# Setup loads on another queue, a first batch computed in pairs of halves, and a convolution split into more and smaller stages

## The chip, the cores and the metric

The kernel runs on one core of a Trainium2 chip. The metric is the device time in microseconds of one execution (us). The core has a matrix engine (PE, with a separate row PEld for its weight loads), a vector engine (DVE), a scalar engine (ACT), a general engine (POOL, GpSimd) and a queue engine (SP) that here only issues transfers (DMAs).

## The reference

The input is x of shape 32 × 96 × 56 × 56 (batch, channel, row, column), all in fp32. Two blocks follow each other.

```python
# block 0
h = depthwise_conv_7x7(x) + conv_b
h = layernorm over channels(h) * ln_g + ln_b
h = gelu(h @ w1 + b1) @ w2 + b2
x1 = h * layer_scale + x
# block 1: two Mamba layers along L = 56*56 tokens of a batch
for i in range(2):
    h = layernorm(seq); xs, z = split(h @ in_w)           # 96 -> 2 x 192
    xc = silu(causal 4-tap conv(xs))
    dt, B, C = split(xc @ xproj_w)                        # 6, 16, 16
    delta = softplus(dt @ dt_w + dt_b)
    state[d, s] = exp(delta*A) * state + delta*B*xc       # scan over tokens, 192 x 16 states
    y = (sum over s of state*C + D*xc) * silu(z)
    seq = seq + y @ out_w
gp = relu(mean of x1 over the picture @ gp_w.T + gp_b)
out = fus_w @ concat(seq, gp) + fus_b
out = batchnorm(out) over batch and picture; return out + x1
```

## The kernel before, in words

The work falls into a prologue, a main part of 256 stages and an epilogue.

**First convolution.** `b0` batches are convolved before the main part starts. `conv_pair(p)` does two channels at a time: a DMA on SP's queue (L160) brings the rows of both channels with all `b0` batches into one of three `xpads`, seven `copy_predicated` of DVE (L165) write a banded 112 × 112 matrix for each of seven column shifts, PE multiplies (L176, two groups of batches with seven taps each), ACT adds the bias (L180), and DMAs store the result in `conv_d[0]` (L184) and the bands in `band_d` (L170), for later use. Three pairs are issued, then the setup of the weights (L189 to L319), then the other 45 pairs. The setup's loads are DMAs on SP's queue: `column`, `blocks` and single ones. Outside the main part a scheduler orders the instructions of each engine; the queue of an engine is served in order.

**First batch.** `block0(0, c, s)` gives the pieces of block 0 for half `s` of chunk `c` (a chunk is 784 tokens, a half 392; four chunks make a batch): `load`, `load_x`, `center` (L365), `square` (L370), `mean` (L375), `root` (L381 and L382: a logarithm and an exponential on ACT), `norm` (L429, DVE), `up` (L434), `gelu` (L442), `down` (L449, L453), `residual` (L460). Each piece has a slot number. For batch 0 these pieces are issued by a sorted list in which each half starts three slots after the one before. Tiles of this part come from a pool with 3 buffers a name and 8 PSUM buffers. ACT's functions come in table sets; `exp_ln_tables()` (L361) preloads the set that has both exponential and logarithm.

**Main part.** A stage is one layer, one batch, one chunk, and the order of the stages alternates between the two layers. It has 24 steps, one for each block of 32 channels (6) and group of states (4). In each step DVE scans (L920), ACT makes the decays (L871), DVE or POOL the inputs (L913, L897), POOL multiplies by C (L924), and PE sums over states into `y` (L957); `spread` (L886, PE) copies `u` to all partitions and `gate` (L938, DVE) multiplies by `z`. The order on PE, ACT, DVE, POOL and SP is written out by hand: `put` places each piece at a slot of a stage and `run` issues it behind, or within, the step of that number. Beside the scan a stage carries the preparation of the next stage (`prep`), the end of the last one (`post`), one half of block 0 for a later batch (`block0`, in stages 2 to 249), and one piece of the remaining convolution: `conv(g, p)`, channel pair p of group g of `NB` batches, in the stages from 2 on. Its first `PARTS` entry has its seven taps (L541) at slots 7.7 to 10.4, the second at slots 18.5 to 22.2; the results are copied by ACT (L554) and stored.

Of the kernel before, what the change touches and what calls it, by code (L numbers as in the profile page):

```python
# [44 lines left out]
C = 96  # L45
# [16 lines left out]
def convnext_mamba_kernel(  # L62
# [31 lines left out]
    nc = tc.nc  # L94
    B = x.shape[0]
# [2 lines left out]
    const = ctx.enter_context(tc.tile_pool(name="const", bufs=1))  # L98


    NB = 7
    b0 = B - 3 * NB if B > 3 * NB else B
    groups = [(0, b0)] + [(b, b + NB) for b in range(b0, B, NB)]
    conv_d = [
        dram.tile([C * H, (hi - lo) * W], F32, name=f"conv_d{lo}", tag=f"conv_d{lo}")
# [18 lines left out]
    for dh in range(7):  # L124
        m = cc.tile([R2, R2], F32, name="m", tag="m", bufs=2)
# [25 lines left out]
    for i in range(3):  # L151
        t = cc.tile([R2, 7, R2], F32, name=f"band{i}", tag=f"band{i}")
        nc.gpsimd.memset(t, 0.0)
        bands.append(t)
        t = cc.tile([R2, b0, W + 6], F32, name=f"xpad{i}", tag=f"xpad{i}")
# [49 lines left out]
    for a in range(2):  # L205
        r = slice(64 * a, 64 * a + 64)
# [12 lines left out]

    def column(src, n, name):  # L220
        t = const.tile([n, 1], F32, name=name, tag=name)
        nc.sync.dma_start(t, src)
        return t

    def blocks(src, name):

        n = src.shape[1]
        t = const.tile([128, NQ, n], F32, name=name, tag=name)
        for a in range(2):
            nc.sync.dma_start(t[64 * a : 64 * a + 64], src.rearrange("(q m) n -> m q n", m=64))  # L230
        return t

    g0, be0 = column(ln0_g, C, "g0"), column(ln0_b, C, "be0")
    b2ls, lsc = column(b2, C, "b2ls"), column(lscale, C, "lsc")
    nc.vector.tensor_tensor(b2ls, b2ls, lsc, ALU.mult)
    b1_sb = const.tile([128, NF], F32, name="b1_sb")
    w2_sb = const.tile([128, NF, C], F32, name="w2_sb")
    ls = su.tile([128, C], F32, name="ls", bufs=1)
    nc.sync.dma_start(ls, lscale.rearrange("c one -> one c").partition_broadcast(128))
    for f in range(NF):  # L240
        nc.sync.dma_start(b1_sb[:, f : f + 1], b1[f * 128 : (f + 1) * 128, :])
        nc.sync.dma_start(w2_sb[:, f, :], w2[f * 128 : (f + 1) * 128, :])
        nc.vector.tensor_tensor(w2_sb[:, f, :], w2_sb[:, f, :], ls, ALU.mult)
    gpw_sb = const.tile([C, C], F32, name="gpw_sb")
    nc.sync.dma_start(gpw_sb, gp_wt)
    gpb = column(gp_b, C, "gpb")
    fw1 = const.tile([C, C], F32, name="fw1")
    nc.sync.dma_start(fw1, fus_wt[0:C, :])
    fw2 = const.tile([C, C], F32, name="fw2")
    nc.sync.dma_start(fw2, fus_wt[C : 2 * C, :])  # L250
    fusb = column(fus_b, C, "fusb")
    bng, bnb = column(bn_g, C, "bng"), column(bn_b, C, "bnb")

# [3 lines left out]
    def norm_weights(dst, src, g, b):  # L257


        n = src.shape[1]  # L260
        raw = su.tile([C, n], F32, name="raw", tag="raw")
        nc.sync.dma_start(raw, src)
        m = su.tile([C, C + 1], F32, name="m", tag="nm")
        nc.vector.tensor_scalar(m[:, 0:C], center_m, g, None, ALU.mult)
        nc.vector.tensor_copy(m[:, C : C + 1], b)
        ps = sups.tile([128, 512], F32, name="ps", tag="nps")
        nc.tensor.matmul(ps[0 : C + 1, 0:n], m, raw, start=True, stop=True)
        nc.vector.tensor_copy(dst, ps[0 : C + 1, 0:n])

    norm_weights(w1_sb, w1, g0, be0)  # L270
    for i in range(2):
        d = {}
        lg, lb = column(ln_g[i], C, f"lg{i}"), column(ln_b[i], C, f"lb{i}")
        wz = const.tile([C + 1, 2 * DIN], F32, name=f"inw{i}", tag=f"inw{i}")
        norm_weights(wz, in_w[i], lg, lb)
        wx = const.tile([C + 1, 4, DIN], F32, name=f"wx{i}", tag=f"wx{i}")
        nc.sync.dma_start(wx, taps[i].partition_broadcast(C + 1))
        for k in range(4):
            nc.vector.tensor_tensor(wx[:, k, :], wx[:, k, :], wz[:, 0:DIN], ALU.mult)
        d["wx"], d["wz"] = wx, wz[:, DIN : 2 * DIN]  # L280
        d["cb"] = blocks(mconv_b[i], f"cb{i}")
        d["xp"] = blocks(xproj_w[i], f"xp{i}")
        d["ow"], d["res"] = blocks(out_w[i], f"ow{i}"), eye
        if i == 1:

            d["res"] = fw1
            for q in range(NQ):
                ps = sups.tile([128, 512], F32, name="ps", tag="nps")
                nc.tensor.matmul(
                    ps[0:C, 0:64], d["ow"][0:64, q, :], ident[0:64, 0:64], start=True, stop=True  # L290
                )
                owt = su.tile([C, 64], F32, name="owt", tag="owt")
                nc.vector.tensor_copy(owt, ps[0:C, 0:64])
                ps = sups.tile([128, 512], F32, name="ps", tag="nps")
                for a in range(2):
                    nc.tensor.matmul(
                        ps[64 * a : 64 * a + 64, 0:C], owt, fw1, start=True, stop=True
                    )
                nc.vector.tensor_copy(d["ow"][:, q, :], ps[:, 0:C])
        d["dtb"] = blocks(dt_b[i], f"dtb{i}")  # L300
        dtw = const.tile([DTR, DIN], F32, name=f"dtw{i}", tag=f"dtw{i}")
        nc.sync.dma_start(dtw, dt_w[i])
        d["dtw"] = dtw
        dcol = blocks(dp[i], f"dp{i}")
        d["D"] = const.tile([128, NQ, 128], F32, name=f"D{i}", tag=f"D{i}")
        for q in range(NQ):
            nc.vector.tensor_scalar(d["D"][:, q, :], ident, dcol[:, q, :], None, ALU.mult)

        ar = su.tile([128, 2 * NQ, NS], F32, name="ar", tag="ar")
        A = const.tile([128, 2 * NQ, NG], F32, name=f"A{i}", tag=f"A{i}")  # L310
        for s in range(4):
            r = slice(32 * s, 32 * s + 32)
            nc.sync.dma_start(ar[r], a_log[i].rearrange("(q m) n -> m q n", m=32))
            nc.scalar.activation(A[r], ar[r, :, s::4], AF.Exp)
        nc.vector.tensor_scalar(A, A, -1.0, None, ALU.mult)
        d["A"] = A
        d["st"] = const.tile([128, 2 * NQ, NG], F32, name=f"st{i}", tag=f"st{i}")
        lay.append(d)
# [5 lines left out]
    for k in range(2):  # L324
        t = const.tile([C + 1, 3 + CH], F32, name=f"hn{k}", tag=f"hn{k}")
        nc.vector.memset(t[C : C + 1, :], 1.0)
        hns.append(t)
        t = const.tile([C + 1, HC], F32, name=f"hz{k}", tag=f"hz{k}")
# [8 lines left out]
    with ExitStack() as main:  # L337
        pre = []
# [6 lines left out]
        def work(shape, name, bufs):  # L345

            pool, n = (pre[0], 3) if pre else (wp, bufs)
            return pool.tile(shape, F32, name=name, tag=name, bufs=n)
# [10 lines left out]
        def exp_ln_tables():  # L359

            nc.scalar.preload_act_table_set("natural_log_exp_and_others")  # L361
# [16 lines left out]
        def rsqrt(ps):  # L378

            rs = ps[0:C, 0:HC]  # L380
            nc.scalar.activation(rs, rs, AF.Ln, bias=eps_c[0:C])  # L381
            nc.scalar.activation(rs, rs, AF.Exp, scale=-0.5)  # L382
# [10 lines left out]
        def block0(b, c, s):  # L393
# [3 lines left out]
            def load():  # L397
                if k == 0:
                    batch_sums[b] = work([C, NCH * 2], "sums", 2)
                v["cv"] = work([C, ROWS, W], "cv", 1)  # L400
                g = 0 if b < b0 else 1 + (b - b0) // NB
                at = (b - groups[g][0]) * W
# [20 lines left out]
                v["ps"] = mean_of(v["sq"], 2)  # L423

            def root():
                rsqrt(v["ps"])

            def norm():
# [10 lines left out]
            def gelu():  # L439
                v["gl"] = work([128, NF, HC], "gl", 1)  # L440
                for f in range(NF):
                    nc.scalar.activation(  # L442
                        v["gl"][:, f], v["pss"][f][:, 0:HC], AF.Gelu, bias=b1_sb[:, f : f + 1]
                    )
                exp_ln_tables()

            def down():
                v["ps"] = psum(2)
# [29 lines left out]
            def fuse():  # L478
# [11 lines left out]
            return last + [  # L490
                (-6, load), (2, load_x), (11.3, center), (12.1, square), (12.4, mean),
                (12.8, root), (14.1, True, norm), (15.6, up), (15.9, gelu), (17.3, down),
                (18.3, residual),
            ]


        with tc.tile_pool(name="p0", bufs=1) as p0, tc.tile_pool(
            name="pp0", bufs=1, space=PSUM
        ) as pp0:
            pre += [p0, pp0]  # L500
            pieces = [
                (slot + 3 * (2 * c + s), piece)
                for c in range(NCH)
                for s in range(2)
                for slot, *_, piece in block0(0, c, s)
            ]
            for _, piece in sorted(pieces, key=lambda p: p[0]):
                piece()
            pre.clear()

        wp = main.enter_context(tc.tile_pool(name="wp", bufs=2))
# [5 lines left out]

        xpad = wp.tile([R2, NB, W + 6], F32, name="xpad", tag="xpad", bufs=1)
        nc.vector.memset(xpad, 0.0)

        PARTS = (0, (NB + 1) // 2), ((NB + 1) // 2, NB)

# [504 lines left out]
    with tc.tile_pool(name="sp", bufs=1) as sp:  # L1027
        n = B * NCH
# [21 lines left out]
    with tc.tile_pool(name="fin", bufs=4) as fin:  # L1050
        for b in range(B):
            for a in range(2):
# [3 lines left out]
                r = fin.tile([C, 2 * CH], F32, name="fr")  # L1056
# [63 lines left out]
```

## Time and profile before

| | |
|---|---|
| three runs | 17344.25 us median, 17338.93 to 17366.62 |
| the profiled execution | 17343.56 us, span 17341.9 us |
| busy share of the span | PE 89%, DVE 93%, ACT 66%, POOL 90% |
| mean granted clock of PE | 0.932 |
| first scan / last scan ends | 574 us / 16980 us |

A row of the profile's groups names line, engine, operation, output and inputs, then busy time and mean duration. PE records two instructions for each fp32 matmul. Times in a timeline are from the start of the span.

### The profile page before, as it was taken

How to read it: one execution, taken by the hardware profiler on the slowest of the kernel's cores; microseconds unless marked ns; L12 is line 12 of the kernel's file. 1: busy time of each engine (PE TensorE's matmuls, PEld its weight loads, DVE VectorE, ACT ScalarE, POOL GpSimd, SP SyncE). 2: the span in 40 equal slices, each digit the busy share in tenths (PEclk: the TensorE clock that was granted, in tenths of full speed). 3: DMA queues.
4: the chain of work that ended last, by engine and by line, in shares of the span. 5: the costliest groups of instructions: out<-in, count | busy, mean ns of one | idle time of the engine just before them, and what ended most of it. 6: DMA issues, size and time to landing. Idle time of an engine off the chain costs nothing. (4 is left out here: it accounts for less than half of the span.)

```text
span 17341.9 us, 217468 instructions
## 1 busy us (share of the span) xinstructions
PE 15452.2 (89%) x67992; PEld 5467.0 (32%) x67992; DVE 16061.7 (93%) x12345; ACT 11459.0 (66%) x18648; POOL 15637.1 (90%) x8737
## 2 busy tenths in 40 slices
PE   8899999999999999999999988888888888888870
PEld 5233333333333333333333322222222222222220
DVE  8699999999999999999999999999999999999994
ACT  1666666666676776666666666666666666666653
POOL 0699999999999999999999999999999999999991
PEclk9899999999999999999999999999999999999985
DMA  4455555555555555555555555555555555555548
GB/s 107 105 138 140 139 136 139 139 140 140 133 141 140 140 140 135 138 140 140 137 136 141 137 129 125 124 131 127 124 126 128 128 125 124 131 128 125 127 113 280
DMA packets 1421981, 2346.44 MB, mean 135 GB/s; under 512 B 629958, under 2 KB 793586, under 8 KB 1420820
## 3 DMA queue, kind: packets, MB, share of 16 engines
q1 hardware_dynamic: 1413652, 2294.00, 53.5%
q10 hardware_dynamic: 7168, 38.54, 0.6%
q8 instruction: 536, 8.78, 0.2%
q14 instruction: 625, 5.12, 0.1%
HBM read 1929.11 MB, written 402.41 MB: 134 GB/s over the span
## 5 line engine op out<-in xcount | busy, mean ns | idle before, releaser
L924 POOL TENSOR_TENSOR da<-h,bc 128x784 f32<-128x784 f32 x6144 | 11295.2, 1861 | 799.0 <-DVE h L920 686.1
L920 DVE TENSOR_TENSOR_SCAN h<-da,st,w 128x784 f32<-128x784 f32 x3072 | 5664.2, 1844 | 324.0 <-ACT st L931 9.4
L957 PE MATMUL y<-da,ssum 128*32 128x392 f32 x24576 | 5131.2, 540 | 429.9 <-POOL da L924 427.5
L913 DVE TENSOR_TENSOR w<-w,bc 128x784 f32<-128x784 f32 x4096 | 3995.7, 976 | 284.0 <-PE w L886 114.6
L897 POOL TENSOR_TENSOR da<-us,bc 128x784 f32<-128x784 f32 x2048 | 3816.3, 1863 | 2.9 <-DMA us<-uu 2.9
L871 ACT ACTIVATE da<-d,A 128x784 f32<-128x784 f32 x4096 | 3757.6, 941 | 43.6 <-DMA d<-dd 27.7
L871 ACT ACTIVATE w<-d,A 128x784 f32<-128x784 f32 x2048 | 1878.8, 918 | 2662.8 <-DVE h L920 2270.2
L920 DVE TENSOR_TENSOR_SCAN h<-w,st,da 128x784 f32<-128x784 f32 x1536 | 2712.4, 1827 | 5.9 <-ACT w L871 4.8
L622 PE MATMUL ps<-hn,wx 97*64 97x392 f32 x12288 | 2262.6, 503 | 7.9 <-DVE hn L610 7.9
L957 PEld LDWEIGHTS y<-da,ssum 128*32 128x32 f32 x24576 | 1093.7, 115 | 3700.0 <-issue 2095.1
L920 DVE TENSOR_TENSOR_SCAN h<-da,w 128x784 f32<-128x784 f32 x1024 | 1827.0, 1784 | 107.9 <-ACT st L931 3.8
L886 PE MATMUL w<-u,sel 64*128 64x392 f32 x4096 | 1028.4, 581 | 638.5 <-DVE h L920 637.4
L622 PEld LDWEIGHTS ps<-hn,wx 97*64 97x64 f32 x12288 | 795.3, 136 | 1429.1 <-issue 1111.3
L701 POOL TENSOR_TENSOR u<-dl,xc 128x784 f32<-128x784 f32 (+1 forms) x512 | 736.8, 1439 | 543.0 <-ACT dl L687 543.0
L951 PE MATMUL y<-xc,D 128*128 128x392 f32 x1536 | 796.6, 604 | 252.1 <-DVE z L938 246.1
L541 PE MATMUL ps<-xpad,band 112*112 112x224 f32 (+1 forms) x4032 | 1003.0, 358 | 0.0
L361 ACT ACT_TABLE_LOAD x759 | 973.8, 1283 | 14.5 <-PEq L1107 0.8
L370 ACT ACTIVATE sq<-ps 96x392 f32<-96x392 f32 x768 | 340.7, 490 | 812.6 <-PE ps L365 464.3
L920 DVE TENSOR_TENSOR_SCAN h<-w,da 128x784 f32<-128x784 f32 x512 | 872.3, 1766 | 0.0
L541 PEld LDWEIGHTS ps<-xpad,band 112*112 112x112 f32 x4032 | 583.8, 175 | 832.5 <-issue 783.5
L679 PE MATMUL ps<-dbl,dtw 6*64 6x392 f32 x3072 | 688.3, 511 | 99.9 <-ACT dbl L657 99.9
L886 PEld LDWEIGHTS w<-u,sel 64*128 64x128 f32 x4096 | 327.7, 196 | 1229.6 <-DVE h L920 1055.3
(124 smaller groups left out, 14412.7 us busy)
## 6 DMA issues: line engine op xcount, KB each, us to landing
bc<-bd SPq DMA_DIRECT2D x4096, 196.0 KB, 5.3
d<-dd SPq DMA_DIRECT2D x6144, 98.0 KB, 2.8
us<-uu SPq DMA_DIRECT2D x2048, 98.0 KB, 2.2
dd<-dl SPq DMA_DIRECT2D x512, 294.0 KB, 3.8
uu<-u SPq DMA_DIRECT2D x1024, 49.0 KB, 1.6
band<-band_d SPq DMA_DIRECT2D x144, 343.0 KB, 3.5
cv<-conv_d SPq DMA_DIRECT2D x256, 147.0 KB, 2.4
xin<-in_x SPq DMA_DIRECT2D x128, 294.0 KB, 3.8
```

The lines of the kernel that those rows point to most:

```text
L361: nc.scalar.preload_act_table_set("natural_log_exp_and_others")
L541: nc.tensor.matmul(v["ps"][0:R2, 0 : (last - first) * W], v["band"][:, dw, :], xpad[:, first:last, dw : dw + W], start=(dw == 0), stop=(dw ...
L622: nc.tensor.matmul(v["x", q][rows(a), 0:HC], weights[:, k, 64 * q : 64 * q + 64], v["hn"][:, o : o + HC], start=(k == 0), stop=(k == last),)
L701: nc.gpsimd.tensor_tensor(S.u[:, lo:hi], v["dl"][:, lo:hi], S.xc[:, lo:hi], ALU.mult)
L871: nc.scalar.activation(e, S.d4[j], AF.Exp, scale=S.d["A"][:, j, g : g + 1])
L886: nc.tensor.matmul(S.u4[:, 512 * a : 512 * a + HC], sel[rows(a), j % 2, :], S.u[rows(a), j // 2, :], start=True, stop=True,)
L897: nc.gpsimd.tensor_tensor(t, S.us[j], S.bcs[g][:, 0, :], ALU.mult)
L913: nc.vector.tensor_tensor(halves(db), S.u4.rearrange("p (a b) -> p a b", a=2)[:, :, 0:HC], halves(S.bcs[g][:, 0, :]), ALU.mult,)
L920: nc.vector.tensor_tensor_scan(ring[:, g, :], S.e.pop((j, g)), db, 0.0 if c == 0 else d["st"][:, j, g : g + 1], ALU.mult, ALU.add,)
L924: nc.gpsimd.tensor_tensor(da, ring[:, g, :], S.bcs[g][:, 1, :], ALU.mult)
L951: nc.tensor.matmul(S.y[:, 0:HC], S.d["D"][:, q, :], S.xc[:, q, :], start=True, stop=False)
L957: nc.tensor.matmul(S.y[r0 : r0 + 32, 0:HC], ssum, da[:, tok(a)], start=False, stop=(g == NG - 1),)
```

## The change

There are three edits. First, all setup loads of the weights (`column`, `blocks`, and the single ones between L239 and L313, 57 DMAs) are issued by GpSimd and no longer by SP. Second, in the first batch both halves of a chunk get the same slots, and a chunk starts four slots after the one before; the table preload stands ahead of the root of each pair instead of behind each gelu, and once behind the whole list. Third, `NB` is 5 in place of 7 and four groups are left for the main part in place of three: the first convolution takes 12 batches (before 11), and the main part carries `conv` in 192 stages with `PARTS` of three and two batches (before 144 stages with four and three).

```diff
-    NB = 7
-    b0 = B - 3 * NB if B > 3 * NB else B
+    NB = 5
+    b0 = B - 4 * NB if B > 4 * NB else B
...
     def column(src, n, name):
         t = const.tile([n, 1], F32, name=name, tag=name)
-        nc.sync.dma_start(t, src)
+        nc.gpsimd.dma_start(t, src)
         return t
...
         for a in range(2):
-            nc.sync.dma_start(t[64 * a : 64 * a + 64], src.rearrange("(q m) n -> m q n", m=64))
+            nc.gpsimd.dma_start(t[64 * a : 64 * a + 64], src.rearrange("(q m) n -> m q n", m=64))
...
-        nc.sync.dma_start(raw, src)
+        nc.gpsimd.dma_start(raw, src)
...
-            nc.sync.dma_start(ar[r], a_log[i].rearrange("(q m) n -> m q n", m=32))
+            nc.gpsimd.dma_start(ar[r], a_log[i].rearrange("(q m) n -> m q n", m=32))
...
             def root():
+                if pre and s == 0:
+                    exp_ln_tables()
                 rsqrt(v["ps"])
...
-                exp_ln_tables()
+                if not pre:
+                    exp_ln_tables()
...
             pieces = [
-                (slot + 3 * (2 * c + s), piece)
+                (slot + 4 * c, piece)
                 for c in range(NCH)
                 for s in range(2)
                 for slot, *_, piece in block0(0, c, s)
             ]
             for _, piece in sorted(pieces, key=lambda p: p[0]):
                 piece()
+            exp_ln_tables()
             pre.clear()
```

The other loads of the setup (`ls`, `b1_sb`, `w2_sb`, `gpw_sb`, `fw1`, `fw2`, `wx`, `dtw`) change their engine in the same way.

More of the change, by code (lines that the diff above doesn't have):

```diff
@@ L238, in convnext_mamba_kernel @@
     ls = su.tile([128, C], F32, name="ls", bufs=1)
-    nc.sync.dma_start(ls, lscale.rearrange("c one -> one c").partition_broadcast(128))
+    nc.gpsimd.dma_start(ls, lscale.rearrange("c one -> one c").partition_broadcast(128))
     for f in range(NF):
-        nc.sync.dma_start(b1_sb[:, f : f + 1], b1[f * 128 : (f + 1) * 128, :])
-        nc.sync.dma_start(w2_sb[:, f, :], w2[f * 128 : (f + 1) * 128, :])
+        nc.gpsimd.dma_start(b1_sb[:, f : f + 1], b1[f * 128 : (f + 1) * 128, :])
+        nc.gpsimd.dma_start(w2_sb[:, f, :], w2[f * 128 : (f + 1) * 128, :])
         nc.vector.tensor_tensor(w2_sb[:, f, :], w2_sb[:, f, :], ls, ALU.mult)
     gpw_sb = const.tile([C, C], F32, name="gpw_sb")
-    nc.sync.dma_start(gpw_sb, gp_wt)
+    nc.gpsimd.dma_start(gpw_sb, gp_wt)
     gpb = column(gp_b, C, "gpb")
     fw1 = const.tile([C, C], F32, name="fw1")
-    nc.sync.dma_start(fw1, fus_wt[0:C, :])
+    nc.gpsimd.dma_start(fw1, fus_wt[0:C, :])
     fw2 = const.tile([C, C], F32, name="fw2")
-    nc.sync.dma_start(fw2, fus_wt[C : 2 * C, :])
+    nc.gpsimd.dma_start(fw2, fus_wt[C : 2 * C, :])
     fusb = column(fus_b, C, "fusb")
@@ L276, in convnext_mamba_kernel @@
         wx = const.tile([C + 1, 4, DIN], F32, name=f"wx{i}", tag=f"wx{i}")
-        nc.sync.dma_start(wx, taps[i].partition_broadcast(C + 1))
+        nc.gpsimd.dma_start(wx, taps[i].partition_broadcast(C + 1))
         for k in range(4):
@@ L301, in convnext_mamba_kernel @@
         dtw = const.tile([DTR, DIN], F32, name=f"dtw{i}", tag=f"dtw{i}")
-        nc.sync.dma_start(dtw, dt_w[i])
+        nc.gpsimd.dma_start(dtw, dt_w[i])
         d["dtw"] = dtw
```

## The prediction

> **What bounds the kernel now.** I read the shares of busy time first (page, part 1): DVE 93%, POOL 90%, PE 89%. No engine is alone at the top, so I cut the span into stretches and read each by itself. The scan of L920 runs 24 times a stage; a count of scans per stretch says that 717 to 9912 us holds 144 stages (those that carry a `conv` piece) and 9912 to 16585 us holds 104 stages without one. The columns are stretch, length, then busy us (instructions) of PE, PEld, DVE, ACT, POOL, then granted TensorE clock, DMA share, GB/s.
>
> ```profile
> core 0: us, PE busy (x) PEld busy (x) DVE busy (x) ACT busy (x) POOL busy (x), PEclk, DMA share, GB/s
> 68.00:101.00 33.00, 6.28 (x26) 2.96 (x24) 18.21 (x39) 2.85 (x10) 0.00 (x0) 0.56 0.29 64
> 101.00:434.00 333.00, 332.03 (x1260) 221.47 (x1260) 302.00 (x295) 46.61 (x90) 0.00 (x0) 0.99 0.45 120
> 434.00:522.00 88.00, 64.56 (x148) 29.76 (x148) 4.62 (x9) 62.69 (x91) 0.00 (x0) 0.81 0.17 44
> 717.00:9912.00 9195.00, 8767.76 (x39240) 3128.24 (x39236) 8762.56 (x6678) 6387.11 (x10512) 8792.00 (x4895) 0.96 0.57 138
> 9912.00:16585.00 6673.00, 5823.71 (x25434) 1929.52 (x25432) 6335.85 (x4824) 4542.83 (x7388) 6345.76 (x3537) 0.93 0.51 127
> ```
>
> Three things are to be seen. From 101 to 434 us, the first convolution, PE is busy 332 of 333 us: PE bounds it. From 68 to 101 PE does almost nothing. In the main part a stage takes 9195 / 144 = 63.85 us with conv work and 6673 / 104 = 64.16 us without: the stages with **more** work are the shorter ones, and their clock is higher (0.96 against 0.93). DVE is busy 60.9 us of a stage in both, so the stage is DVE's work plus its waits. The waits of DVE in the two stretches (line waited, releaser, us in total, times, longest), with conv work and then without:
>
> ```profile
> DVE w L913 <- PE w L886: 94.5, 157, 2.3
> DVE z L938 <- PE y L957: 19.6, 17, 1.2
> ```
> ```profile
> DVE hz L429 <- ACT ps L382: 95.1, 76, 2.3
> ```
>
> With conv work DVE waits for a PE that is behind (0.79 us a stage); without it, for the normalisation chain of `block0` (0.91 us a stage). Why that chain is late shows one stage of each kind, over the same part of the stage:
>
> ```profile
> 1381.70:1386.80 5.10, 5.10 (x24) 2.15 (x20) 5.10 (x4) 3.38 (x6) 5.10 (x4) 1.00 0.42 121
> 13398.90:13404.00 5.10, 1.28 (x8) 0.14 (x4) 5.10 (x4) 3.70 (x5) 5.10 (x4) 1.00 0.45 132
> 13404.00:13410.80 6.80, 6.50 (x12) 2.71 (x12) 6.53 (x7) 3.01 (x6) 6.59 (x4) 0.52 1.05 226
> ```
>
> With taps PE is busy all 5.10 us; without them 1.28 us, and in the next 6.8 us the granted clock is 0.52, just when the matmuls L365 and L375 that feed `hz` run.
>
> [...]the trace has the 1283 ns and nothing behind it (a load at 454.66, its ACTIVATE at 455.96), so I price a load at 1.28. [...]
>
> **Part 1, setup loads on GpSimd's queue, and 12 batches in the first convolution.** Now 57 setup DMAs stand in SP's queue ahead of the fourth pair's input:
>
> ```profile
> 97.53 0.32 SPq L160 DMA_DIRECT2D xpad<-in_x x1
> 100.90 332.13 PE L176 MATMUL ps<-xpad,band 112*112 112x336 f32 x1260 [2.43 <-DMA xpad<-in_x]
> ```
>
> PE stands from 68 to 100.9 for it. With the loads gone from SP, that DMA follows the three first ones, and of the 33 us only the setup matmuls (some 5 us) stay: −28. Each pair grows from 616 to 672 columns: 332.13 / 45 = 7.38 us, times 672/616 = 8.05; 48 pairs × 0.67 = +32. DVE's seven COPY_PREDICATED (7 × 1.04 = 7.3 us a pair) stay below that. Net +4.
>
> Moving them has a price. In the instruction order of the changed kernel PE's first matmul, L267, needs the 19th GpSimd load; DVE waits for the 53rd and, by way of four ACT exponentials of `A`, the 57th in the middle of the fifth pair's band. Behind that wait stand the remaining band copies, behind them PE. GpSimd is free for it (no instruction from 10 us to past 522), and gets to the loads at about 9 us. With p us per load, the last has landed at 9 + 57p + 2; the fifth pair's band is ready 6 us later and PE wants it at about 80 us; more setup work of DVE in the sixth pair adds some 4 us once DVE is late. p isn't in the trace. At p = 1.0 the last lands at 68 and the band is ready at 74: no stall, and below that nothing is gained beyond the gap already counted. At 2.0 it is 125 + 6 − 80 + 4 = 55 us. [...]**Sum of part 1: +12, between +2 and +60.**
>
> **Part 2, halves in pairs.** ACT today, for one half of the first batch:
>
> ```profile
> 454.66 1.28 ACT L381 ACT_TABLE_LOAD   x1
> 455.96 0.55 ACT L381 ACTIVATE ps<-ps,eps_c 96x392 f32<-96x392 f32 x1
> 456.53 1.28 ACT L442 ACT_TABLE_LOAD   x1
> 457.82 0.59 ACT L442 ACTIVATE gl<-ps,b_sb 128x392 f32<-128x392 f32 x1
> 458.43 1.28 ACT L382 ACT_TABLE_LOAD   x1
> 459.72 0.47 ACT L382 ACTIVATE ps<-ps 96x392 f32<-96x392 f32 x1
> ```
>
> Four loads a half, 25 in all (the preload of L361 stands once at 0.8 us, where it does nothing for this stretch, and the order of the changed kernel leaves it there). Changed, ACT loads for the exponential line, the logarithm line and the gelu line once a pair: 10 in all, 15 × 1.28 = 19 us less. The period of a pair is now 2 × 10.44 (454.66 to 506.85 is five halves) = 20.9 us. The new one, by its chain: `norm`, then a cv load (2.7 us, because 3 buffers leave the next chunk's second half waiting for this chunk's `norm`), one L365 0.7, six L434 4.1 (6 records take 2.14 us at 454.43) with the last gelu 0.6 behind, two loads 2.6, two logarithms 1.1, two exponentials 0.9 with `norm` 0.55: about 13 us. Three periods give 3 × 7.9 = 24. Bounds: 12, if PE's clock stays near 0.8 and the chain stretches, and 30. **−24.**
>
> **Part 3, 192 conv stages of five batches.** A stage's taps are 14 + 14 matmul records of 224 and 168 columns; they become 168 and 112. The view of PE's order in one stage gives the price of 56 columns: four records of 224 take 0.95 us (1382.29 to 1383.24), four of 168 take 0.75:
>
> ```profile
> 1418.90 0.83 PE L541 MATMUL ps<-xpad,band 112*112 112x168 f32 x4
> 1419.65 0.85 PE L957 MATMUL y<-da,ssum 128*32 128x392 f32 x4
> 1420.44 0.54 PE L541 MATMUL ps<-xpad,band 112*112 112x168 f32 x2
> 1420.91 0.93 PE L886 MATMUL w<-u,sel 64*128 64x392 f32 x4
> ```
>
> So 0.05 us a record, 0.7 us a part. The second part stands directly ahead of the L886 for which DVE waits, in a PE without a gap: that wait, 0.60 us on average (94.5 / 157), becomes shorter by up to 0.7. The long ones (to 2.3) keep the rest, and the z wait comes ahead of most taps of that part and stays. I take 50 of the 94.5: 0.35 us a stage, bounds 0 and 94. The 48 stages that newly carry taps go from 64.16 to 63.85 − 0.35 = 63.5: −32; bounds −5 and −45. Their extra ACT copies, DMAs (343 KB of band each) and SP issues lie beside the scans: the 144 stages carry the same now, with DMA share 0.57. Each group's stores end before its first batch is read (last conv stage 193, first stage that reads the last group 210). **−82, between −5 and −139.**
>
> **Sum.** +12 − 24 − 82 = −94. The profiled execution took 17343.56 us (span 17341.9 and 1.7 around it): 17249.6. The median, 17344.25, is 0.7 above it: **17250**.
>
> **Rivals.** About 0.2% (35 us) is what a measurement of this kernel can tell from no change.
> (a) Slower: the shorter taps no longer hold the clock. Then every conv stage would pay the 0.91 us of `hz` and keep its 0.79: 144 × 0.91 + 48 × 0.79 = +169, less 12 for the prologue: 17500.[...] Against it: from 5.10 busy us some 12 records × 0.05 = 0.6 go, which leaves 88%. 8%.
> (b) GpSimd issues at 2 us a load: 48 us more than I count, 17298. From p = 2.8 on (stall 102) nothing of the gain would be left. The unknown p speaks for it, the idle GpSimd against. 15%.
> (c) The waits for PE come from clock drops and not from the taps: the first 144 stages gain nothing, the 48 gain 0.31 each: −15 − 24 + 12, 17317. The long waits speak for it. 15%.
> (d) All of the 94.5 goes and GpSimd is quick: 17250 − 44 − 8 = 17198. 7%.
> Likeliest 55%, its own range 17215 to 17285.
>
> Range 17180 to 17335, which leaves out (a) and the tails. Faster by over 0.2% (below 17310): the likeliest, (d), most of (b), a little of (c): 0.74. Within: 0.14. Slower: 0.12.
>
> **What would show it.** Right: L176 without a gap near 68 to 101 us; ten table loads between the first `sq` and `gp`; `hz L429 <- ACT ps L382` near zero up to stage 193; `w L913 <- PE w L886` about halved per stage; mean stage near 63.5. Wrong: a clock near 0.93 in conv stages, DVE or ACT waiting on GpSimd's loads beyond 100 us, or stages at 63.85.

## The result, and the profile after

The changed kernel takes 17310.74 us (median of 12 runs, 17287.2 to 17319.6), the kernel before, run beside it, 17358.96 (12 runs, 17338.93 to 17373.69): ratio 0.997, interval 0.9962 to 0.9978, about 48 us less. The forecast was 94 less, from a median of 17344.25. The profiled execution took 17305.15 us, 38.4 less than the profiled one of before; executions of one kernel spread over some 30 us.

Where the 38.4 us came from, by the scans of the two traces:

| | before | after | moved | forecast |
|---|---|---|---|---|
| last matmul of the first convolution | 432.6 | 442.1 | +9.5 | +12 |
| from there to the first scan | 141.6 | 119.6 | −22.0 | −24 |
| first scan to end of the last | 16406.2 | 16377.0 | −29.2 | −82 |
| after the last scan | 361.4 | 364.7 | +3.3 | 0 |

The prologue did what its sum said; the miss lies in the main part. First the changed kernel's stretches, with the columns known from before; the first three rows are stages 2 to 145, 146 to 193 (taps only now) and 194 to 249 (no taps in either kernel):

```profile
core 0: us, PE busy (x) PEld busy (x) DVE busy (x) ACT busy (x) POOL busy (x), PEclk, DMA share, GB/s
706.30:9887.70 9181.40, 8603.89 (x39240) 3074.87 (x39236) 8766.01 (x6679) 6375.89 (x10514) 8792.22 (x4895) 0.96 0.56 137
9887.70:12948.70 3061.00, 2866.08 (x13080) 1025.23 (x13078) 2921.80 (x2227) 2123.89 (x3505) 2931.07 (x1633) 0.96 0.56 137
12948.70:16543.50 3594.80, 3138.51 (x13696) 1038.72 (x13694) 3412.07 (x2597) 2445.79 (x3978) 3417.57 (x1905) 0.93 0.52 127
68.00:101.00 33.00, 29.88 (x104) 17.11 (x103) 28.46 (x44) 3.98 (x9) 0.02 (x1) 0.90 0.36 97
```

In stages 2 to 145 PE is busy 164 us less than before (8767.76), yet the stretch is only 14 us shorter: 63.76 us a stage, before 63.855. The 48 new conv stages went from 64.144 to 63.771. The last row is the hole that PE had before: 29.88 of 33 us are now filled.

DVE's waits in the first of these stretches (line waited, releaser, us in total, times, longest), then in the second:

```profile
DVE hz L431 <- ACT ps L382: 33.4, 23, 1.8
DVE w L917 <- PE w L890: 32.5, 38, 2.3
DVE z L942 <- PE y L961: 18.0, 16, 1.2
...
DVE hz L431 <- ACT ps L382: 12.2, 7, 1.8
DVE w L917 <- PE w L890: 9.0, 12, 1.1
```

The wait for `w` fell from 94.5 to 32.5 us, more than the forecast 50. But a wait that conv stages didn't have before is there now: `hz`, 33.4 us in 23 stages and 12.2 us in 7, some 1.5 us each. It is the wait of the stages without taps.

One of these stages, stage 16, shows how it comes. PE in order of time (start, us, line, operation, count, in brackets the idle time before it and its releaser):

```profile
1623.02 0.83 PE L545 MATMUL ps<-xpad,band 112*112 112x168 f32 x4
1624.86 0.85 PE L961 MATMUL y<-da,ssum 128*32 128x392 f32 x4 [1.01 <-POOL da L928]
1625.64 0.83 PE L545 MATMUL ps<-xpad,band 112*112 112x168 f32 x4
1627.13 1.68 PE L890 MATMUL w<-u,sel 64*128 64x392 f32 x4 [0.66 <-DVE h L924]
1628.73 2.93 PE L365 MATMUL ps<-seq,center_m 96*96 96x392 f32 x4
```

The same place in stretches, then DVE's `hz` of this stage, and after that the same place of a stage of the kernel before (stage 40):

```profile
1623.70:1627.10 3.40, 1.76 (x10) 0.70 (x8) 3.40 (x3) 2.99 (x5) 3.40 (x3) 1.00 0.83 219
1627.20:1634.00 6.80, 6.80 (x12) 2.63 (x12) 6.53 (x6) 3.18 (x6) 6.59 (x4) 0.50 1.03 222
```
```profile
1637.97 0.56 DVE L431 TENSOR_TENSOR hz<-cv,ps 96x392 f32<-96x392 f32 x1 [1.84 <-ACT ps L382]
```
```profile
3171.70:3175.10 3.40, 2.68 (x12) 1.24 (x12) 3.40 (x3) 2.99 (x5) 3.40 (x3) 1.00 0.85 240
```

Before, the taps kept PE behind POOL's products `da`, and in this stretch it waited for DVE alone (0.70 us ahead of L886): 2.68 of 3.40 us busy. Now it also waits 1.01 us for POOL, is busy 1.76 of 3.40 us, and the granted clock is 0.50 for the next 6.8 us. In these, L890 takes 1.68 us (0.93 in the stage shown of before) and the normalisation's L365 2.93 (1.56 before); DVE stands 1.84 us for `hz`. As means over stages 2 to 145, PE's wait for POOL in the 6 us ahead of this L890 rose from 0.08 to 0.62 us, its wait for DVE from 0.36 to 0.62.

Counted over the trace's clock records, 31 drops start between 26 and 30 us of a stage in stages 2 to 193, of 3.41 or 6.83 us each; 30 of these 192 stages have a `hz` wait, and all 30 have such a drop. In the kernel before, stages 2 to 145 have no such drop and no `hz` wait.

The prologue's lines. ACT, for one pair of halves of the first batch:

```profile
474.56 1.28 ACT L444 ACT_TABLE_LOAD   x1
475.86 2.98 ACT L444 ACTIVATE gl<-ps,b_sb 128x392 f32<-128x392 f32 x6
478.85 1.28 ACT L381 ACT_TABLE_LOAD   x1
480.15 1.03 ACT L381 ACTIVATE ps<-ps,eps_c 96x392 f32<-96x392 f32 x2
481.19 1.28 ACT L382 ACT_TABLE_LOAD   x1
```

Three loads a pair, ten in all, and the next pair's L381 load at 491.68: a period of 12.8 us, forecast 13. In the main part L381 and L382 have no load of their own (the last is at 548.1 us): there one of L361, 1.28 us, stands ahead of both. PE's first matmuls, and a load of GpSimd's queue:

```profile
46.40 1.57 PE L267 MATMUL ps<-raw,m 96*97 96x384 f32 x2 [46.40 <-DMA raw<-in_w]
```
```profile
23.50 0.53 POOL L242 DMA_DIRECT2D w_sb<-in_w  x1 [9.40 <-DMA g<-in_ln_g]
```

A load costs GpSimd 0.5 to 0.6 us of issue in most cases (0.71 at most), half of the 1.2 that I had put down, an estimate for which the trace of before had no figure. But by then GpSimd had stood four times (9.40, 6.27, 6.42 and 2.52 us) until an earlier load had landed, and PE starts at 46.4 us, before at 43.9.

### The profile page after: what moved, and what is told of

Read it like the earlier page. It is cut to its first block, busy times and chain, and to the rows that moved or that the text cites. A ratio compares the mean times of both kernels' runs of the same rounds, so it can differ in the third digit from the quotient of the medians.

```text
span 17303.4 us, 220582 instructions
## 1 busy us (share of the span) xinstructions
PE 15491.8 (90%) x69336; PEld 5545.3 (32%) x69336; DVE 16067.7 (93%) x12345; ACT 11456.8 (66%) x18729; POOL 15672.2 (91%) x8794
## 5 line engine op out<-in xcount | busy, mean ns | idle before, releaser
L890 PE MATMUL w<-u,sel 64*128 64x392 f32 x4096 | 1019.7, 576 | 632.7 <-DVE h L924 631.8
L545 PE MATMUL ps<-xpad,band 112*112 112x168 f32 (+1 forms) x5376 | 1086.7, 312 | 0.0
L545 PEld LDWEIGHTS ps<-xpad,band 112*112 112x112 f32 x5376 | 709.8, 175 | 1088.3 <-issue 1028.7
L890 PEld LDWEIGHTS w<-u,sel 64*128 64x128 f32 x4096 | 325.4, 195 | 1145.3 <-DVE h L924 1017.4
```

The source lines that it names most:

```text
L545: nc.tensor.matmul(v["ps"][0:R2, 0 : (last - first) * W], v["band"][:, dw, :], xpad[:, first:last, dw : dw + W], start=(dw == 0), stop=(dw ...
L890: nc.tensor.matmul(S.u4[:, 512 * a : 512 * a + HC], sel[rows(a), j % 2, :], S.u[rows(a), j // 2, :], start=True, stop=True,)
```

## The experiments

**Theory N**: in stages with taps the shorter first part lets PE run dry between 24 and 28 us of a stage, the clock falls to half (0.50 in stage 16), the normalisation is late, and DVE waits for `hz`. Its rivals stand in the expectations. "Idle" below is PE's mean idle time from 24.0 to 28.5 us of a stage (counted from its first scan), and "drops" the clock drops that start at 26 to 30 us, both from the trace, for stages 2 to 145; the waits are DVE's, in us, with their number.

| kernel | parts (batches) | idle | drops | `hz` | `w` | stage |
|---|---|---|---|---|---|---|
| before | 4 + 3 | 0.44 | 0 | 0 | 94.5 (157) | 63.855 |
| after | 3 + 2 | 1.24 | 23 | 33.4 (23) | 32.5 (38) | 63.760 |
| NB = 5 alone | 3 + 2 | 1.23 | 20 | 23.7 (17) | 26.0 (33) | 63.700 |
| four and one | 4 + 1 | 0.70 | 0 | 0 | 27.2 (48) | 63.424 |
| two and three | 2 + 3 | 1.53 | 16 | 18.5 (15) | 81.1 (140) | 63.949 |
| overlap | 4 + 2 | 0.68 | 0 | 0 | 31.8 (41) | 63.476 |
| seven with fill | 4 + 3 | 0.52 | 0 | 0 | 89.8 (157) | 63.831 |
| seven, five and two | 5 + 2 | 0.21 | 0 | 0 | 51.3 (59) | 63.545 |

**Third edit alone.** The kernel before with `NB = 5` and four groups.

> The kernel before with NB = 5 alone (12 batches first, 192 conv stages; setup loads on SP and halves one by one as before). If the edits add up: first scan 32 us later than before (48 pairs x 0.67), main part 29 us shorter, total within 10 us of before. If the main part's gain hangs on the other edits[...], the main part keeps 16406 us and the total is 30 us above before.

Measured: 17329.31 us, 0.9982 (0.9975 to 0.999). First scan 605.7 us, 31.5 later, as expected for the twelfth batch; the main part 44 us shorter. So the edit does gain in the main part, with the same new `hz` wait. The total, expected within 10 us of before, is 31 less in the median and 10 less in the profiled execution. The main part, of the same code, is 15 us shorter than in the changed kernel, which shows how far single executions differ.

**Parts of four and one** (the first part back to 224 columns).

```diff
-        PARTS = (0, (NB + 1) // 2), ((NB + 1) // 2, NB)
+        PARTS = (0, 4), (4, NB)
```

> The changed kernel with PARTS (0,4),(4,5): first part's taps 224 columns as before the change, second part's 56 (changed kernel: 168 and 112). Theory N (the first part's taps fill PE between 21 and 28 us of a stage; when they are short, [...]the clock halves and the normalisation chain reaches DVE late): hz<-ACT ps in the 192 conv stages falls from 45.6 us (33.4 + 12.2) to below 5, w<-PE w falls from 41.5 to 15 to 30 because the second part is shorter still; total about 17260, 50 below the changed kernel. Rival M (the hz wait has to do with [...]later transfers, not with the length of the taps): hz stays between 30 and 60 us, total 17290 to 17310.

Measured: 17249.77 us, 0.9938 (0.9925 to 0.995), 61 us less than the changed kernel with the same taps in all. DVE's waits in stages 2 to 145:

```profile
DVE w L917 <- PE w L890: 27.2, 48, 1.8
DVE z L942 <- PE y L961: 12.3, 11, 1.2
```

`hz` is gone from the list, and no drop starts at 26 to 30 us, as theory N says.

**Parts that overlap.** `PARTS = (0, 4), (3, NB)`: the fourth batch is computed twice, with the same values.

> The changed kernel with PARTS (0,4),(3,5): the fourth batch is convolved twice, so the first part has 224 columns and the second keeps 112. PE gets 0.7 us a stage more work than in the changed kernel. N: hz falls below 5 us, w<-PE w stays at 30 to 55; total about 17270, faster although PE does more. M: nothing gained, hz 30 to 60 us, total 17310 or up to 20 more.

Measured: 17253.56 us, 0.9939 (0.9925 to 0.9953). PE does **more** than in the changed kernel and the time is 57 us less: the first part's length counts, not PE's work. `w` stays at 31.8, the value of a second part of two batches.

**Parts of two and three.** `PARTS = (0, 2), (2, NB)`.

> The changed kernel with PARTS (0,2),(2,5): first part 112 columns, second 168. N: hz<-ACT ps in the 192 conv stages rises from 45.6 us to 100 or more, w<-PE w rises to about 0.6 us a stage as before the change (110 to 125 us); total 17420 to 17480. M: hz stays near 45, w rises by the same; total about 17390.

Measured: 17338.44 us, 0.9989 (0.9981 to 0.9998), below both forecasts. In stages 2 to 145:

```profile
DVE w L917 <- PE w L890: 81.1, 140, 2.3
DVE z L942 <- PE y L961: 21.6, 19, 1.2
DVE hz L431 <- ACT ps L382: 18.5, 15, 1.8
```

`w` is back near its value of before, as a second part of three batches should make it. But `hz` did not grow; in this, N's forecast failed. The idle time rose only from 1.24 to 1.53 us, and the drops did not rise with it (23 and 16). Why PE found other work for the rest of the missing taps isn't settled.

The clock records show what decides. In each of the three traces below, the starts of the drops lie on one grid of 3.413 us, to 0.001 us. "Window" is here one step of this grid. Take the windows that run at full clock and end 26 to 30 us into one of stages 2 to 193, and count those with the half clock behind them, by PE's busy share in the window:

| kernel | under 0.50 | 0.50 to 0.55 | 0.55 to 0.60 | 0.60 and over |
|---|---|---|---|---|
| after | 17 of 17 | 13 of 15 | 1 of 13 | 0 of 178 |
| two and three | 11 of 11 | 9 of 9 | 0 of 7 | 0 of 195 |
| four and one | none | 0 of 1 | 0 of 5 | 0 of 214 |

So at this place it is the busy share within one window that counts (in the changed kernel 30 of the 32 windows under 0.55 have a drop behind them, and 1 of the 191 others), not columns. How many windows meet the gap is a matter of how the grid falls on the stages: 42 windows end at 27.6 to 28.4 us of a stage in the changed kernel, 31 of them with a drop behind, and only 25 with parts of two and three, 20 with a drop. Why fewer meet it there isn't known.

**The first two edits alone**, each in the kernel before.

> The kernel before with the first edit alone: the setup's 57 loads on GpSimd's queue, still 11 batches, pieces of the first batch and NB = 7 as before. By the sum of part 1 without its +32 for the twelfth batch: the 28 us gap of PE goes and some 5 us come back as a later start and short waits, so the last L176 at about 410 us (before 432.6), the first scan at about 552 us (574.2), and the whole time 22 us below before, 17338. The main part isn't touched: 64.0 us a stage and w<-PE w near 94 us in stages 2 to 145. Rival: GpSimd's loads hold up the bands as long as SP's queue held up the input, then the first scan stays within 5 us of 574.

Measured: 17338.74 us, 0.9991 (0.9982 to 1.0). Last matmul of the convolution 410.3 us, first scan 555.6: −18.6.

> The kernel before with the second edit alone: halves of the first batch in pairs, one change of tables a pair. If the prologue gains what the table loads say, 15 loads of 1.28 us and the shorter chain: the first scan at about 552 us (before 574.2), last L176 unchanged at 433, the whole time 22 us below before, 17338. Together with the first edit alone (-22) and NB = 5 alone (+31.5 at the first scan) that adds up to the -12.5 of the changed kernel. Rival: the gain comes only when PE's clock is up or the weights are there earlier, then less than 10 us here.

Measured: 17334.23 us, 0.9989 (0.9982 to 0.9996). First scan 550.0: −24.2. With the +31.5 of the third edit that makes −11.3 at the first scan, against −12.5 measured together. In the prologue the edits add, and each of these two is about as large as its step said. The whole times moved less (−14 and −18): in the profiled executions the untouched main part was 11 and 18 us longer than in that of before, and the wait for `w` in stages 2 to 145 grew from 94.5 to 104.9 and 111.4 us. Why is not known.

**A fill where no taps are left.** Parts of four and one, and in stages 194 to 249 a piece `fill` with seven matmuls at the slots of the first part:

```diff
+        def fill():
...
+                        v["ps"] = psum(2)
+                    nc.tensor.matmul(
+                        v["ps"][0:R2, 0 : 4 * W], held[0][:, dw, :],
+                        xpad[:, 0:4, dw : dw + W], start=(dw == 0), stop=(dw == 6),
+                    )
...
                 put(m, conv(*convs[m - 2]))
+            elif 2 <= m < len(halfs) + 2:
+                put(m, fill())
```

> The changed kernel with parts of four batches and one, and in the 56 stages that have block 0 but no convolution left (194 to 249) the first part's seven taps of four batches computed once more with the last band and input at the same slots; nothing reads these products, and no load, copy or store goes with them. Theory N (PE idle at 24 to 28 us of a stage lets the clock fall, and the slow matmuls of the normalisation make DVE wait for hz): idle there falls from 2.9 us to 0.7, no clock drop starts at 24 to 30 us of these stages, the hz wait of 51.2 us is below 5, the stage goes from 64.17 to about 63.55 as in the 48 stages before it, and the whole time falls by some 35 us to 17215, although PE does 3 us more work a stage. Rival R (hz is late for its own order of pieces or its buffers): hz stays near 51 us and the stages at 64.17 or longer, 17250 to 17280.

Measured: 17196.07 us, 0.9909 (0.9894 to 0.9924). The stretch of stages 194 to 249, to be held against the third row of the changed kernel above, and its longest wait:

```profile
12893.70:16435.50 3541.80, 3222.76 (x14482) 1112.44 (x14482) 3406.84 (x2597) 2455.84 (x3980) 3418.89 (x1905) 0.97 0.53 129
```
```profile
DVE w L937 <- PE w L910: 3.0, 5, 1.7
```

PE works 84 us more and the stretch is 53 us shorter; the clock goes from 0.93 to 0.97, and 52.3 us of `hz` wait are gone with nothing in their place. PE's idle time falls from 2.94 to 0.76 us, and of 54 drops that started at 24 to 30 us of these stages none is left. A stage takes 63.25 us, less than the expected 63.55. This is the clearest test of N: the same stages with the same work, and products that nobody reads beside it.

**The convolution's bias.** Two versions on top of the fill. The first only moves the two bias loads (L147, 4-byte elements) behind the first three inputs.

> The same with the convolution's bias, two loads of 4-byte elements that SP issues in 2.2 and 10.3 us ahead of the first inputs, issued behind the first three inputs. If the band copies wait for the weights and inputs that stand behind and beside these transfers (the copies start at 27.4 us, PE at 46.4, GpSimd's loads land up to 15 us after issue), everything up to the first scan comes 10 to 15 us earlier: first scan at about 551 us (563.7 with the parts of four and one), the whole time about 17203. Rival: the setup's order on DVE and GpSimd sets the start (GpSimd's first load is issued at 8.8 us and the last some 57 us later), then less than 4 us come.

Measured: 17187.22 us, 0.9905 (0.989 to 0.992), but the first scan is at 564.1 us: nothing of the expected 10 to 15 us came in the prologue. The band copies did start at 15.2 us in place of 27.4, but `raw<-in_w` landed even later and PE started at 52.5. The 9 us less lie behind the first scan (in the profiled executions 13 us less in the main part and 6 after it), where the code is the same, and are not explained. The second version loads whole rows and picks the even or the odd channel (`low` is 1 in the first `H` rows, 0 in the others):

```diff
-        nc.sync.dma_start(
-            cb[j * H : (j + 1) * H].unsqueeze(2), bv[j].partition_broadcast(H)
-        )
...
+    nc.sync.dma_start(call, conv_b.rearrange("c one -> one c").partition_broadcast(R2))
...
+    pair = call.rearrange("q (p two) -> q two p", two=2)
+    nc.vector.tensor_tensor(cb, pair[:, 0, :], pair[:, 1, :], ALU.subtract)
+    nc.vector.tensor_scalar(cb, cb, low, None, ALU.mult)
+    nc.vector.tensor_tensor(cb, cb, pair[:, 1, :], ALU.add)
```

> The kernel with parts of four and one and with the fill, its convolution bias loaded as 112 whole rows of 384 bytes (one load) and picked by three short DVE operations, in place of 5376 elements of 4 bytes. Theory E: these elements hold up the loads beside and behind them, both SP's inputs and GpSimd's setup loads (raw<-in_w landed 17.6 us after issue). Then the band copies start near 15 us, the setup loads land within some 6 us, PE starts near 30 us in place of 46, the last first-convolution matmul comes near 430 us (445.0), the first scan near 550 us (565.4), and the whole time falls to about 17181. Rival: GpSimd's own queue sets the start, since it waits for landings of loads issued before; then PE still starts after 42 us and the first scan stays within 4 us of 565.

Measured: 17164.4 us, 0.9891 (0.9876 to 0.9905), first scan 534.7: −30.7, twice what was expected. PE's first matmul, and the issue of the load that it waits for:

```profile
22.80 1.57 PE L274 MATMUL ps<-raw,m 96*97 96x384 f32 x2 [22.80 <-DMA raw<-in_w]
```
```profile
20.23 0.51 POOL L269 DMA_DIRECT2D raw<-in_w  x1
```

By the view of DMA issues it lands 2.4 us after issue; in the changed kernel it was 17.6, with the bias loads only moved 15.9. So the 5376 elements of 4 bytes held up GpSimd's loads wherever they stood in SP's order. The changed kernel's trace has 263667 packets of 4 bytes, this one 258279, 5388 fewer: about one packet an element. And the price fell on another queue's loads.

**Seven batches again.** The fill and the first two edits, with the third undone, parts of four and three; then with parts of five and two.

> The kernel with the fill, but with the third edit undone: seven batches a group, 11 batches in the first convolution, parts of four and three in stages 2 to 145, the fill in stages 146 to 249. By the sum of what was measured: first scan 31.5 us earlier, stages 2 to 145 back to 63.86 us (w<-PE w near 95 to 105 us, no hz), stages 146 to 249 at 63.25 as with the fill: 17196 - 31 + 144 x 0.41 - 48 x 0.27 = 17211. If instead the split in fours groups did something else for these 48 stages, more than 17225.

Measured: 17226.08 us, 0.9925 (0.991 to 0.994), 15 over the sum and just past the 17225 of the alternative; the profiled execution took 17207.97. By stages it is nearer the sum: 63.831 us in 2 to 145, 63.430 and 63.204 in the two filled stretches (63.25 expected), `w` at 89.8. The whole time alone does not tell the two apart.

> As the one before, with parts of five and two. Theory W: what DVE waits for in w<-PE w is set by the columns of the second part, which stands directly ahead of the spread; with 112 columns it falls to about 32 us as in the changed kernel (32.5 with parts of three and two, 31.8 with parts that overlap), hz stays at 0 since the first part is long, stages 2 to 145 go to about 63.45, and the whole time to about 17150. Rival T: the wait is set by the whole of PE's work in a stage, seven batches either way; then it stays near 95 us and the time at 17211. A first part of 280 columns may also make the normalisation late by its length; that would show as hz waits without clock drops at 26 to 30 us.

Measured: 17173.91 us, 0.9896 (0.9879 to 0.9912), 24 over the expected 17150. PE has the same work in both; moving one batch out of the second part takes `w` from 89.8 to 51.3 us. Rival T falls; W has the direction, but 51.3 is not the expected 32, so the columns of the second part alone don't set it. No drops at 26 to 30 us and no `hz` wait: 280 columns aren't too long.

**Put together**: seven batches, five and two, the fill, the bias in rows.

> The two best versions put together: seven batches a group with parts of five and two, the fill in the 104 stages without convolution, and the convolution's bias loaded as whole rows. If prologue and main part add: first scan near 502 us (531.1 less the 30 that whole rows brought), main part as with parts of five and two (63.55 and 63.25 us a stage), the whole time 17174 - 27 = 17147. If eleven batches in the first convolution leave the later loads less cover, the first scan comes later than 510 us and the whole time stays near 17164, that of the version with five batches a group.

Measured: 17134.3 us (17132.14 to 17138.96), 0.9874 (0.9858 to 0.9891), first scan 501.9. It beats both kernels, by 220 us and by about 176. With the fill and the bias in rows, groups of five (parts of four and one) take 17164.4 us: the split no longer pays beside parts of five and two, since the fill holds the clock in stages 146 to 193 as well, and the twelfth batch costs 32 us in the first convolution.

What is left: in the kernels of the table PE also idles 1.5 to 1.7 us at 36 to 40 us of a stage, and a drop starts behind it in 20 to 33 of stages 2 to 145. A fill at that place wasn't tried. Most drops start elsewhere, though. In the kernel before, 127 of the 159 drops of stages 2 to 145 start at 8 to 16 us of a stage, and there PE was 88 to 100% busy in the window ahead of them (after: 107 of 157, 87% and over). Stage 20 of the kernel before, the window and what follows it:

```profile
1877.41:1880.82 3.41, 3.33 (x14) 1.35 (x14) 3.31 (x4) 3.33 (x7) 3.41 (x3) 1.00 0.10 29
1880.83:1884.20 3.37, 3.37 (x17) 1.03 (x18) 3.20 (x3) 3.06 (x4) 3.15 (x3) 0.50 0.37 78
```

About three quarters (72%) of PE's time in these windows is L679, matmuls whose operands have 6 rows (6*64 and 6x392). So busy time alone doesn't hold the clock. Whether the few rows are the reason, and what these drops cost, no run here tests.

## Why the prediction was right or wrong

**Part 1, right in the sum.** The gap closed (SP issues the fourth pair's input at 57.13 us, before at 97.53) and the twelfth batch cost 31.8 us (442.1 after, 410.3 with eleven). With eleven batches the last matmul came 22.3 us earlier (432.6 to 410.3), where −28 + 8 says 20. The +8 for stalls was an estimate at 1.2 us a load of GpSimd's (9 + 57 × 1.2 + 2 = 79.4; 79.4 + 6 − 80 is 5, and part of the 4), a price that no trace had shown. So its size was near, the mechanism not: an issue took half of that price, while the time went into the landing of loads beside the bias's small elements (17.6 us for `raw<-in_w`). That a price too high and a delay left out nearly cancel is luck. The fifth pair's bands never held PE up for long (one gap of 3.12 us at 78).

**Part 2, right.** −24 forecast, −24.2 with the edit alone; period and number of loads as said.

**Part 3, wrong: a new wait was put at nothing.** The 144 stages moved by −14 us where −50 was forecast, the 48 new ones by −18 where −32 was. The step on `w` stood up: forecast −50, measured −62, set mostly by the part ahead of the spread. The term that was mis-sized is the one that I put at nothing in the likeliest case and argued away in rival (a): "from 5.10 busy us some 12 records × 0.05 = 0.6 go, which leaves 88%". I took out only the records inside the stretch. But PE was behind POOL there, and each shorter tap before it let PE catch up; PE's idle time rose by 0.80 us at one place (0.44 to 1.24), about the 0.7 us of all seven taps, and it is spent waiting for POOL and DVE. In the stage shown 1.76 of 3.40 us stay busy, 52% and not 88%. Rival (a) was thus right in its mechanism and wrong in its extent: it hits 30 of 192 stages, not all, because the idle time must fall into one window of the 3.413 us grid. The `hz` waits cost 33.4 + 12.2 = 45.6 us of the 53 that the main part missed its forecast by, and with the parts of four and one they are gone. Taken off, they leave 63.53 and 63.52 us a stage, where the prediction said 63.5.

Nor does a drop need a PE that idles as much as in the stage without taps that the prediction shows (1.28 of 5.10 us busy): of the 31 drops counted above, 14 follow windows in which PE was 50 to 60% busy.

The remainder is not settled. In stages 2 to 145 the waits that the profile names fell by 30 us (−62, +33.4, −1.6), the stretch by 14 only; by the windows DVE's idle time fell by 17 us (432.4 to 415.4).

Of the signs that I named, `w` fell to a third and the table loads came true; `hz` near zero and a stage near 63.5 did not. The sign I had set for a clock failure, a mean clock near 0.93 in conv stages, did not show (0.96), since drops in every sixth stage hardly move the mean (23 of the 157 drops in stages 2 to 145; before, 159 in all). The whole time, 17310.74, lies near the 17317 of rival (c), by luck: (c) fails as the main cause, since with the split of the taps alone `w` goes from 32.5 to 81.1 us (two and three) and from 89.8 to 51.3 (five and two).

## What to carry to other kernels

Removing work from an engine that isn't the bound can cost time, when that work kept its clock up (here 45.6 us of `hz` waits): look for the engine's idle time within one window (3.413 us in these traces) ahead of the chain that ends last, and count everything that lets it catch up, not only what stands in the window. A mean over all stages hides this: here 31 drops in 192 stages made the cost. What a moved load costs can lie in what else is in flight more than in the issuing engine (17.6 us to landing, 0.51 of issue). Where a wait is short and rare, cut the trace by stage.

## What the runs showed of the hardware

- The granted clock falls to half (0.50) without any long idle stretch: in stage 16 of the changed kernel it fell behind idle times of 1.01 and 0.66 us, at 1.76 of 3.40 us busy. At 26 to 30 us of stages 2 to 193 of the changed kernel, all 17 windows (of 3.413 us) under 0.50 busy have the half clock behind them, and none of 178 at 0.60 or over.
- A busy share near 1 did not hold the clock: behind windows 88 to 100% busy, mostly with matmuls of 6 rows, the clock fell 127 times in stages 2 to 145 of the kernel before.
- Matmuls whose products nobody reads paid for themselves here: 84 us more PE work made 56 stages 53 us shorter.
- A load from GpSimd's queue took 0.5 to 0.7 us to issue; beside 4-byte elements of another queue one landed 17.6 us after issue, without them 2.4.
